# Moving the routing steps of the layer-1 context attention by one pair of heads

## The chip, the cores and the metric

The kernel runs on one core of a Trainium2 chip. The metric is the device time of one execution in microseconds (us), and the lower the better. Five engines work side by side, each taking its own instructions strictly in the order in which they were queued: TensorE (PE, matrix products, with its weight loads listed apart as PEld), VectorE (DVE), ScalarE (ACT), GpSimd (POOL) and SyncE (SP, which only starts transfers). They wait for each other through semaphores. The order on every engine is fixed when the kernel is built.

## The reference, cut to what matters

The program is a decoder of four layers (L0 to L3), each with a self-attention, a cross-attention to a context and a feed-forward part, on x of shape 8 batches x 256 rows x 256. The part that matters is the cross-attention of L1 and the beginning of what follows it:

```
q = x Wq + bq,  k = ctx Wk + bk,  v = ctx Wv + bv       # 16 heads of 64; ctx has 77 rows per batch
s = q k^T / 8,  masked keys replaced by a large negative number
p = softmax(s);  o = p v
x = layernorm(x + concat(o) Wo + bo)                     # the "new x" of the batch
# L1 feed-forward: a mixture of 8 experts, 2 per row, each with a limited capacity
r = rms-scaled x;  probs = softmax(r W_router);  top 2 of 8
rank of each row in its expert = number of earlier rows that chose that expert
rows with rank < capacity are scattered to their expert's slots
```

The routing of a batch needs that batch's new x, and, for the ranks, the counts of all batches before it.

## The kernel before

The cross-attention of L0 and of L1 is one function, `cross64` (L849); `bias` is true for L1 alone. It walks over the eight batches b = 0 to 7. A batch has two tiles of 128 rows (t = 0, 1) and eight pairs of heads (n = 0 to 7). For each batch it goes through these stages:

1. `weights(b)`: 64 matmul instructions on L919 make the scores of 16 heads. ScalarE copies them (L932), VectorE masks them (L933), takes the maximum (L939) and subtracts it (L940), ScalarE takes the exponential (L899), VectorE sums and inverts (L901, L902), and POOL (t = 0) or VectorE (t = 1) multiplies (L903). This is the tile P.
2. Three of the next batch's query projections q (L156, from xt and w), the values V of the batch (L156, from w and cT), and the output projection of the batch before (L156, from w and oT, two groups of 16 instructions). `finish` (L279) adds that to x (L281) and starts the layer norm: statistics (L253, L255), the inverse root on POOL (L183, L184), and the new tile x (L264).
3. `outputs(b)`: the loop over the eight pairs n. Each turn takes the next query projection if one is left (five turns have one, and in the last batch none), perhaps a "tick", the product po of the turned probabilities with V (L970), and the transposes of P for pair n + 2 (L955, four instructions), which ScalarE or VectorE copy into PT (L144 or L142). Two pairs are turned before the loop. oT and q are copied out with their bias by ScalarE (L151) and VectorE (L149) in turn.

Below, T(n) is the group of transposes for pair n, PT(n) its copy, q(n) the query projection taken in turn n, po(n) and oT(n) the product of turn n and its copy.

A tick advances the oldest entry of a list of generators. At the end of a batch `put_both` is put on that list, and it puts `Routing.batch` behind itself. So the four ticks of `outputs(b)`, for b = 1 to 7, do four things for batch b - 1, in this order:

- first tick: two transposes of each of the two tiles of the new x (L236), copied to xt by VectorE and ScalarE;
- second tick: the router's matmuls (L156, from rw and xt) and the chain of small operations behind them: scores (L2576), maximum (L2578), subtraction (L2579), exponential on ScalarE (L2580), sum (L2581), reciprocal (L2582), scaling (L2583), top values and their places (L2586, L2587, L2588), the one-hot rows rhot (L2594), their sum rsel (L2597) and the running counts rbefore (L2600);
- third tick: nothing, an empty step;
- fourth tick: the matmuls with the tiles `upper` and `onesb` (L156) that count the earlier rows, from rsel and rbefore, the ranks (L2609, L2611) and slots (L2615 to L2620), and four scatters on POOL (L1041).

The ticks stand ahead of the turn's po. In the first batch the list is empty, so nothing happens there.

The queue order is not the order of the text in every place: a scheduler chooses, at build time, where among the copies each small operation of VectorE and ScalarE stands. The squares for the root mean square (L2554), though issued by the second tick, stand far ahead of it on ScalarE.

## Time and profile before

| what | us |
|---|---|
| time, median of 3 runs | 3500.77 (3495.93 to 3503.63) |
| the profiled execution's own time | 3466.69 |
| its span, first to last instruction | 3465.0 |
| mean granted TensorE clock | 0.913 |
| one full batch of the L1 context attention, start of L919 to the next | 34.28 |
| TensorE busy in it | 32.63 |
| VectorE busy in it | 27.89 |

The profile is that of one execution, which was 34 us shorter than the median of the runs. Busy times of an engine count instructions in flight, and a TensorE that is shown busy may run at half clock; the granted clock stands beside it in the table of windows. Idle time is shown in square brackets with what ended it.

### The profile page before, as it was taken

How to read it: one execution, taken by the hardware profiler on the slowest of the kernel's cores; microseconds unless marked ns; L12 is line 12 of the kernel's file. 1: busy time of each engine (PE TensorE's matmuls, PEld its weight loads, DVE VectorE, ACT ScalarE, POOL GpSimd, SP SyncE). 2: the span in 40 equal slices, each digit the busy share in tenths (PEclk: the TensorE clock that was granted, in tenths of full speed). 3: DMA queues.
4: the chain of work that ended last, by engine and by line, in shares of the span. 5: the costliest groups of instructions: out<-in, count | busy, mean ns of one | idle time of the engine just before them, and what ended most of it. 6: DMA issues, size and time to landing. Idle time of an engine off the chain costs nothing. (4 is left out here: it accounts for less than half of the span.)

```text
span 3465.0 us, 49405 instructions
## 1 busy us (share of the span) xinstructions
PE 3068.0 (89%) x19135; PEld 2169.0 (63%) x19146; DVE 1819.0 (52%) x4852; ACT 1055.4 (30%) x2386; POOL 911.1 (26%) x1370
## 2 busy tenths in 40 slices
PE   4777679989998998998999999898888998888789
PEld 3444357768886666665566776565555886676556
DVE  7887556641005656785111221576675344777652
ACT  4666422222222233332111111343222112344211
POOL 2222323343313211232000000322343454322241
PEclk6777779989999999999999999999777999988899
DMA  9900110025532000001010333100002562000000
GB/s 334 333 1 6 34 42 16 16 94 185 187 128 89 17 28 14 17 17 59 14 37 25 113 131 118 37 20 8 7 19 84 200 210 77 25 1 7 13 6 19
DMA packets 132672, 241.58 MB, mean 70 GB/s; under 512 B 14600, under 2 KB 103952, under 8 KB 124752
## 3 DMA queue, kind: packets, MB, share of 16 engines
q1 hardware_dynamic: 108176, 138.34, 11.8%
q0 software_dynamic: 23104, 98.95, 8.3%
q8 instruction: 155, 2.54, 0.3%
q10 hardware_dynamic: 1152, 1.05, 0.1%
q14 instruction: 85, 0.70, 0.1%
HBM read 158.61 MB, written 79.69 MB: 69 GB/s over the span
## 5 line engine op out<-in xcount | busy, mean ns | idle before, releaser
L156 PE MATMUL ps<-xt,w 128*128 128x256 f32 (+1 forms) x1408 | 444.6, 465 | 8.3 <-issue 8.3
L156 PE MATMUL ps<-w,hT 128*128 128x256 f32 (+1 forms) x1792 | 397.4, 380 | 0.0
L156 PEld LDWEIGHTS ps<-w,hT 128*128 128x128 f32 (+1 forms) x1792 | 330.5, 187 | 55.9 <-issue 6.0
L156 PE MATMUL ps<-gT,w 128*128 128x256 f32 (+1 forms) x1472 | 356.9, 401 | 5.7 <-ACT gT L144 3.0
L156 PEld LDWEIGHTS ps<-xt,w 128*128 128x128 f32 x1408 | 263.8, 194 | 150.5 <-issue 129.8
L156 PEld LDWEIGHTS ps<-gT,w 128*128 128x128 f32 x1472 | 276.8, 191 | 76.1 <-ACT gT L144 3.9
L156 PE MATMUL ps<-w,oT 128*128 128x256 f32 x768 | 184.1, 394 | 12.3 <-DVE oT L1423 11.2
L156 PEld LDWEIGHTS ps<-w,oT 128*128 128x128 f32 x768 | 147.7, 196 | 48.6 <-issue 12.6
L1147 ACT ACTIVATE hT<-ps,more 128x256 f32<-128x256 f32 x152 | 71.9, 473 | 199.1 <-PE ps L156 199.1
L236 PE MATMUL ps<-ident,x 128*128 128x128 f32 x320 | 64.8, 314 | 74.2 <-DVE x L264 57.3
L276 POOL TENSOR_TENSOR xb<-x,rows 128x256 f32<-128x256 f32 x96 | 74.0, 778 | 212.7 <-DVE res L281 205.5
L264 DVE TENSOR_SCALAR x<-res,mv,rs 128x256 f32<-128x256 f32 x128 | 58.8, 459 | 123.0 <-POOL rs L184 123.0
L1158 DVE COPY y<-ps 128x512 f32<-128x512 f32 x41 | 28.3, 690 | 174.6 <-PE ps L156 174.6
L1224 DVE TENSOR_TENSOR hT<-hT,ps 128x512 f32<-128x512 f32 x56 | 38.5, 687 | 150.6 <-PE ps L156 150.6
L686 ACT ACTIVATE e<-ps,nm 128x128 bf16<-128x128 f32 (+1 forms) x256 | 103.7, 459 | 40.1 <-DVE nm L681 24.1
L1220 ACT ACTIVATE hT<-ps 128x512 f32<-128x512 f32 x56 | 33.4, 597 | 238.5 <-PE ps L156 238.5
L1717 POOL TENSOR_TENSOR kpad<-kpad,rows 128x256 f32<-128x256 f32 (+1 forms) x10 | 7.3, 729 | 363.5 <-DVE hu L1666 276.2
L236 PEld LDWEIGHTS ps<-ident,x 128*128 128x128 f32 x320 | 39.5, 155 | 98.9 <-DVE x L264 44.9
L903 POOL TENSOR_TENSOR P<-P,z 128x1232 f32<-128x1232 f32 (+1 forms) x32 | 55.2, 1734 | 167.3 <-DVE z L902 167.3
L970 PE MATMUL ps<-PT,V 77*64 77x256 f32 x512 | 90.8, 413 | 6.9 <-ACT PT L144 4.4
L1581 ACT ACTIVATE f<-ps,neg 128x512 f32<-128x512 f32 x128 | 77.3, 688 | 57.7 <-PE ps L1578 57.7
L1582 DVE SCALAR_TENSOR_TENSOR f<-ps,f 128x512 f32<-128x512 f32 x128 | 79.1, 682 | 26.1 <-ACT f L1581 26.1
(665 smaller groups left out, 6344.7 us busy)
## 6 DMA issues: line engine op xcount, KB each, us to landing
l2x<-zero SPq DMA_DIRECT2D x28, 1024.0 KB, 11.4
l0x<-zero SPq DMA_DIRECT2D x16, 1024.0 KB, 11.4
w<-in_L_ffn_rg SPq DMA_DIRECT2D x8, 1024.0 KB, 7.1
w<-in_L_ffn_ru SPq DMA_DIRECT2D x8, 1024.0 KB, 5.0
w<-in_L_ffn_rd SPq DMA_DIRECT2D x8, 1024.0 KB, 5.4
l2e<-y SPq DMA_DIRECT2D x22, 256.0 KB, 2.3
rows<-in_rows SPq DMA_DIRECT2D x9, 544.0 KB, 3.7
l0e<-y SPq DMA_DIRECT2D x19, 256.0 KB, 2.7
```

The lines of the kernel that those rows point to most:

```text
L156: self.nc.tensor.matmul(out, lhsT, rhs, start=(i == 0), stop=(i == last))
L236: self.nc.tensor.transpose(ps[:, k * P : (k + 1) * P], x[:, k * P : (k + 1) * P], self.ident)
L264: nc.vector.tensor_scalar(t, r, mv[:, 0:1], rs, ALU.subtract, ALU.mult)
L276: self.nc.gpsimd.tensor_tensor(t, self.X[i], row, ALU.add)
L686: nc.scalar.activation(e[:, : (t + 1) * P], ps[j][:, i, :], AF.Exp, bias=nm[:, t, h : h + 1], accum_out=z[:, t, h : h + 1],)
L903: eng.tensor_tensor(pr, pr, z.unsqueeze(2).to_broadcast([P, n, SC]), ALU.mult)
L970: nc.tensor.matmul(po[64 * m : 64 * m + 64, :S], V[:, h * 64 : (h + 1) * 64], ahead[n % 2][:, m, :], start=True, stop=True,)
L1147: nc.scalar.activation(hT[:, f + m, :], ps[:, m * 256 : (m + 1) * 256], func, bias=more[:, f + m : f + m + 1])
L1220: nc.scalar.activation(hT[:, f, :], ps, func, **({"bias": bias(f)} if bias else {}))
L1224: nc.vector.tensor_tensor(hT[:, f, :], hT[:, f, :], ps, ALU.mult)
L1581: nc.scalar.activation(f[:, j], ps[j], AF.Exp, bias=neg1)
L1582: self.mark = nc.vector.scalar_tensor_tensor(f[:, j], ps[j], 1.0, f[:, j], ALU.max, ALU.min)
```

## The change

The four ticks of a batch are taken in other turns of the loop in L1: turns 2, 4, 5 and 7 in the place of 1, 3, 5 and 7. L0 keeps its turns. The first and the second tick so come one pair later, the empty third and the fourth stay where they were.

```diff
@@ cross64, outputs
                 for n in range(8):
                     next(between, None)
-                    if n % 2:
+                    if n in ((2, 4, 5, 7) if bias else (1, 3, 5, 7)):
                         self.tick()
                     po = self.ps()
```

No instruction is added or removed. In the built order POOL's and SyncE's queues are the same as before; those of TensorE, ScalarE and VectorE differ in `outputs` of batches 1 to 7. The two copies to xt change engines (the first tile's goes to VectorE, the second's to ScalarE), since the copies take turns.

VectorE's queue from the router's scores to the counts, in batches 1 to 6, before and after:

```
before: L2576, oT(3), L2578, L2579, L2581, L2582, L2583, L2586, L2587, L2588, L2594, PT(6), L2597, PT(7), L2600, oT(6), L2600
after:  oT(3), L2576, L2578, L2579, PT(6), L2581, L2582, PT(7), L2583, oT(6), L2586, L2587, L2588, L2594, L2597, L2600, L2600
```

In batch 7, before and after:

```
before: L2576, L2578, PT(5), L2579, PT(6), L2581, L2582, PT(7), L2583, oT(6), L2586, L2587, L2588, L2594, L2597, L2600, L2600
after:  PT(5), L2576, L2578, PT(6), L2579, PT(7), L2581, oT(6), L2582, L2583, L2586, L2587, L2588, L2594, L2597, L2600, L2600
```

(The small steps for the experts' weights, L2630, L2633 and L2634, are left out here; they stand between L2587 and L2600.)

## The prediction

> **What bounds the kernel now.** I read the page first, then the table of windows by batch, then TensorE's waits in this stage, then the timeline of a middle batch and of the last one. The page and the window of batch 2 (the columns are PE, PEld, DVE, ACT, POOL busy, then granted clock and DMA):

> ```profile
> PE 3068.0 (89%) x19135; PEld 2169.0 (63%) x19146; DVE 1819.0 (52%) x4852; ACT 1055.4 (30%) x2386; POOL 911.1 (26%) x1370
> ...
> 1398.65:1432.93 34.28, 32.63 (x217) 23.42 (x217) 27.89 (x86) 13.25 (x30) 10.56 (x13) 1.00 0.05 17
> ```

> TensorE is busy for 32.63 of 34.28 us, at full clock, and no transfer matters (DMA share 0.05). So a batch costs what TensorE's queue costs. TensorE's waits from 1375 to 1606 us:

> ```profile
> PE ps L236 <- DVE x L264: 9.6, 6, 1.6
> PE ps L970 <- ACT PT L144: 4.4, 1, 4.4
> PE ps L156 <- DVE rsel L2597: 1.9, 1, 1.9
> ```

> The first line is what the change aims at: six batches in which the transposes of the new x wait 1.6 us for x. The third is one wait, in the last batch, for rsel. In the timeline of batch 2:

> ```profile
> 1419.02 0.66 DVE L142 COPY PT<-ps 77x512 f32<-77x512 f32 x1
> ...
> 1419.19 0.38 PE L236 MATMUL ps<-ident,x 128*128 128x128 f32 x2
> ...
> 1420.72 0.41 DVE L264 TENSOR_SCALAR x<-res,mv,rs 128x256 f32<-128x256 f32 x1 [0.95 <-POOL rs L184]
> ...
> 1421.19 0.44 PE L236 MATMUL ps<-ident,x 128*128 128x128 f32 x2 [1.61 <-DVE x L264]
> ...
> 1423.60 0.65 PE L970 MATMUL ps<-PT,V 77*64 77x256 f32 x4
> ...
> 1430.23 0.66 PE L955 MATMUL ps<-ident,P 128*77 128x128 f32 x4
> 1430.82 0.65 PE L970 MATMUL ps<-PT,V 77*64 77x256 f32 x4
> 1431.40 0.18 PE L156 MATMUL ps<-rsel,upper 128*128 128x8 bf16 x1
> ...
> 1432.93 3.80 PE L919 MATMUL ps<-l1kT,qT 64*128 64x77 f32 x64
> ```

> The first tile is ready and the second is 1.61 us late. The lines from 1430.23 are T(7), po(6), the counting matmul of rsel and the next scores: no wait there now. VectorE's rsel ended 0.59 us before its matmul (1430.65 + 0.16, against 1431.40).

> **What the change takes away.** Without the transposes, turn 1 goes on to po(1), T(3), q(2). They are 2.04 us apart per turn (1423.60 less 1421.56, po(2) less po(1) now). But po(1) needs PT(1), which VectorE copies from 1419.02 for 0.66 us, behind the first x and its statistics. TensorE would reach po(1) at 1419.19 and can start it at about 1419.74 (0.06 us for the semaphore, as from x's end at 1421.13 to 1421.19): a new wait of 0.55. Then T(3) at 1420.32, q(2) at 1420.82, the transposes at 1421.69. Both tiles have been ready since 1421.13, so they take 0.49 and po(2) starts at 1422.2, not 1423.60. The gain is 1.4 us on TensorE at this point. The two xt copies change engines; that costs nothing, for their readers, the router's matmuls, come two turns later (about 4 us).

> Going on, T(7) starts at 1430.23 - 1.4 = 1428.85, as router and pair 3 only change places.

> **What it adds.** The router's matmuls end as before plus one pair, and the counting matmul stays in turn 7. Between them TensorE now has po(4), T(6), po(5), T(7), po(6), about 2.9 us; before, po(3), T(5) and q(4) lay between as well, 2.04 us more. VectorE's queue for this is PT(6), L2581, L2582, PT(7), L2583, oT(6), L2586 and so on to L2597, and the in-order engine cannot start L2583 before T(7) is done and copied. That order has run already: from PT(7) to rsel it is the order of batch 7 before the change (T(7), PT(7), then VectorE's steps, then the counting matmul):

> ```profile
> 1599.65 0.66 PE L955 MATMUL ps<-ident,P 128*77 128x128 f32 x4
> ...
> 1600.35 0.69 DVE L142 COPY PT<-ps 77x512 f32<-77x512 f32 x1 [0.21 <-PE ps L955]
> 1600.96 0.16 DVE L2583 TENSOR_TENSOR rs<-rs,rm 128x16 f32<-128x16 f32 x1
> ...
> 1602.53 0.17 DVE L2597 TENSOR_TENSOR rsel<-rhot 128x16 bf16<-128x16 f32 x1
> ...
> 1602.77 0.18 PE L156 MATMUL ps<-rsel,upper 128*128 128x8 bf16 x1 [1.87 <-DVE rsel L2597]
> ```

> T(7) to counting matmul: 1602.77 - 1599.65 = 3.12 us, with 1.87 us of TensorE idle. Taken over, the counting matmul comes at 1428.85 + 3.12 = 1431.97, against 1431.40: every batch from 1 to 6 loses 0.57 us net, having gained 1.4 and lost 1.97. Behind that wait stand po(7) and the 64 score instructions; ScalarE and VectorE wait for these, and the whole softmax of the next batch hangs on them, so the loss is carried one for one. Six batches: 3.4 us. POOL's four scatters start after the slots and follow; POOL then waits another 4.04 us for L903's input (1408.96), so they stay covered; uncovered, four of 1.27 us would show. In batch 7 no x was late; there L2582 and L2583 now stand behind oT(6), two dependent steps of about 0.2 us more: 0.4. Sum at full clock: +3.8 us.

> **The clock.** These windows of 3.41 us are TensorE busy, granted clock, DMA:

> ```profile
> 1557.19:1560.61 3.42, 2.29 (x14) 1.00 0.00 0
> ...
> 1601.57:1604.98 3.41, 2.21 (x12) 1.00 0.00 0
> 1604.98:1608.39 3.41, 3.41 (x10) 0.50 0.11 38
> ...
> 2434.42:2437.83 3.41, 3.41 (x40) 0.50 0.00 0
> 2437.83:2441.25 3.42, 1.98 (x40) 0.50 0.02 5
> ```

> The clock changes only at the edges of such windows. The first row holds most of an x wait and is followed by full clock; the second holds the end of the rsel wait, tiny matmuls and po(7), and half clock follows. Busy time alone does not tell them apart. Weighting each matmul's streaming time by its rows over 128 does: in the first row projections and transposes fill 0.58 of the window, in the second po(7) has 77 rows and the counting matmuls stream 8 columns, 0.35. Over all windows of this trace at full clock, I get no fall above about 0.42 beyond a few strays, and hardly any stay below 0.36. The other way, the fourth row is full of work and the clock does not return: half of it is 32-row matmuls. By the same sum, windows at half clock return above about 0.75. All these shares are my estimates, from instruction shapes and start times.

> For the new wait: a window with 1.9 us idle keeps 1.5 us for T and po (about 0.8 by this measure) or po(7) and L919 (about 0.45 to 0.5), so 0.15 to 0.35, mostly a fall. It takes effect near the start of L919. L919 has 64 rows, so by the estimate it cannot bring the clock back; 3.8 us of scores become 7.6, and only a window of projections, V and output projection ends it. That is two or three windows, 6.8 to 10.2 us at half clock, so 3.4 to 5.1 us lost. Of this 0.55 comes back, since TensorE then reaches PT(1) late. TensorE carries the rest, not VectorE: the first half of P was ready at 1412.7 (L903, 1411.93 + 0.78), 2.7 us before T(0) at 1415.4. With 2.5 windows: 4.25 - 0.55 = 3.7 per batch; for six batches 22, if nearly all fall.

> [...] The 1601.57 row shows a fall with at most 1.9 us idle in one piece, so I go by the row.

> **Sum.** 3.8 + 22 = +26 us. The profiled execution would go from 3466.69 to about 3493. The median of the runs is 34 us longer for reasons the profile doesn't show; I add the same 26 to it: 3500.8 + 26 = 3527.

> **Rivals.**
> - *The clock falls for one window only, or seldom.* If L919's pairs count as full activity, one window costs 1.7 - 0.55 = 1.15 us; with the 3.8: +10.7, about 3511. With no fall at all +3.8, about 3505. For it: the six x waits of 1.6 us never cost the clock. Against: those stand among 128-row projections, the new wait between 77-row and 64-row work.
> - *Faster.* The rsel chain costs nothing new, because TensorE's next po's and VectorE's copies move apart enough. Then 1.4 us times six is gained: -8.4, about 3492. It decides for faster where the new wait is under 1.4 us. Against: the queue order and the 3.12 us above, of which over 1 us are ten small operations that cannot overlap.
> - *The change doesn't remove the wait*, since the second x is late for turn 2 too. It would need x 0.6 us later than now; then about +11 with no fall in clock, near the first rival.

> **How the numbers follow.** Lasting fall of the clock 0.62. It gives from 3.8 + 3 x 2.85 = +12 (half of the six batches fall, for two windows) to 3.8 + 6 x 5.1 = +34 (all fall, for three windows, and nothing comes back). One window or seldom, +3.8 to +12, 0.25; faster 0.10; the rest 0.03. The range from 3503 to 3538 takes both of the first two cases, with 1 us below and 3 above for the spread of the runs (3495.93 to 3503.63), and leaves out the faster one. A measurement of this kernel tells about 0.2%, 7 us. Slower by more: 0.62 and 0.16 of the 0.25. Within: the other 0.09 and the 0.03. Faster: 0.10.

> **What would show it.** After: TensorE's waits list x (L264) no longer for L236 in six batches, PT(1) some 0.5 us each for L970 if the batch was not slowed, and rsel seven times near 1.9 us. The windows after each show 0.50 under L919, and its instructions last near 7 us. A batch lasts about 38.5 us, not 34.28. I am wrong on the clock if L919 stays at 3.8 us, and wrong on the chain if rsel waits are under 1.4 us.

## The result and the profile after

The change makes the kernel slower: 3523.68 us median of 7 runs (3510.92 to 3528.57) against 3500.77 for the kernel before, ratio 1.0065 [1.0049, 1.0082], or +22.9 us. The profiled execution took 3523.71 us (span 3522.0, mean granted clock 0.898, against 0.913).

The line of the page with the busy times, which answers to that of before:

```profile
PE 3121.0 (89%) x19135; PEld 2202.5 (63%) x19146; DVE 1817.7 (52%) x4852; ACT 1056.0 (30%) x2386; POOL 911.5 (26%) x1370
```

The window of the same batch in the kernel after, from one start of L919 to the next (columns as before):

```profile
1409.01:1449.36 40.35, 38.48 (x217) 28.18 (x217) 28.01 (x86) 13.24 (x30) 10.77 (x13) 0.84 0.04 14
```

The instructions are the same (217 matmul instructions in both windows; VectorE, ScalarE and POOL are busy as long as before to within 0.3 us), but TensorE is busy for 38.48 us instead of 32.63, at a mean clock of 0.84 instead of 1.00. The batch lasts 40.35 us; of the four that follow three take 40.48 to 40.65 and the last 38.65. TensorE's waits from 1375 to 1660 us (total, times, longest):

```profile
PE ps L156 <- DVE rsel L2597: 13.4, 7, 2.2
PE ps L970 <- ACT PT L144: 2.2, 1, 2.2
PE ps L970 <- DVE PT L142: 0.3, 1, 0.3
```

The line for x is gone, and rsel is waited for seven times instead of once. TensorE's timeline around the end of a batch:

```profile
1396.35 0.60 PE L236 MATMUL ps<-ident,x 128*128 128x128 f32 x4
...
1404.10 0.65 PE L970 MATMUL ps<-PT,V 77*64 77x256 f32 x4
1406.62 0.19 PE L156 MATMUL ps<-rsel,upper 128*128 128x8 bf16 x1 [1.87 <-DVE rsel L2597]
...
1406.80 1.12 PE L970 MATMUL ps<-PT,V 77*64 77x256 f32 x2
...
1409.01 7.11 PE L919 MATMUL ps<-l1kT,qT 64*128 64x77 f32 x64
```

All four transposes of x run in one piece without a wait. The counting matmul waits 1.87 us, and from there on everything takes about twice as long: each of the two groups of po(7) 1.12 us instead of 0.65, the 64 score instructions 7.11 us instead of 3.80. The windows of 3.41 us at the end of the next batch (TensorE busy, clock, DMA) show where the clock goes and when it is back:

```profile
1443.65:1447.06 3.41, 1.54 (x15) 1.00 0.00 0
1447.06:1450.48 3.42, 3.42 (x18) 0.50 0.00 0
...
1460.71:1464.13 3.42, 3.42 (x10) 1.00 0.03 3
```

The first row holds the rsel wait; half clock follows for four windows, 1447.06 to 1460.71. That the clock changes only at such edges holds for both traces: its 135 changes in the kernel before and its 149 in the kernel after lie on one even grid of 3.413 us, none more than 0.01 us off it.

### The profile page after: what moved, and what is told of

It is laid out like the page before. It is cut to its first block, busy times and chain, and to the rows that moved or that the text cites. A ratio compares the mean times of both kernels' runs of the same rounds, so it can differ in the third digit from the quotient of the medians.

```text
span 3522.0 us, 49419 instructions
## 1 busy us (share of the span) xinstructions
PE 3121.0 (89%) x19135; PEld 2202.5 (63%) x19146; DVE 1817.7 (52%) x4852; ACT 1056.0 (30%) x2386; POOL 911.5 (26%) x1370
## 5 line engine op out<-in xcount | busy, mean ns | idle before, releaser
L156 PE MATMUL ps<-xt,w 128*128 128x256 f32 (+1 forms) x1408 | 455.4, 474 | 7.7 <-issue 7.7
L156 PE MATMUL ps<-w,hT 128*128 128x256 f32 (+1 forms) x1792 | 397.4, 379 | 0.0
L156 PEld LDWEIGHTS ps<-xt,w 128*128 128x128 f32 x1408 | 270.7, 199 | 152.8 <-issue 128.9
L156 PE MATMUL ps<-gT,w 128*128 128x256 f32 (+1 forms) x1472 | 357.2, 400 | 9.9 <-issue 3.9
L156 PEld LDWEIGHTS ps<-w,hT 128*128 128x128 f32 (+1 forms) x1792 | 329.9, 186 | 56.5 <-issue 6.0
L156 PEld LDWEIGHTS ps<-gT,w 128*128 128x128 f32 x1472 | 276.1, 191 | 81.4 <-issue 4.3
L156 PE MATMUL ps<-w,oT 128*128 128x256 f32 x768 | 185.6, 396 | 12.2 <-DVE oT L1423 11.1
L156 PEld LDWEIGHTS ps<-w,oT 128*128 128x128 f32 x768 | 148.5, 197 | 49.3 <-issue 14.1
L236 PE MATMUL ps<-ident,x 128*128 128x128 f32 x320 | 62.0, 307 | 65.1 <-DVE x L264 48.1
L264 DVE TENSOR_SCALAR x<-res,mv,rs 128x256 f32<-128x256 f32 x128 | 56.6, 443 | 118.8 <-POOL rs L184 118.8
L1224 DVE TENSOR_TENSOR hT<-hT,ps 128x512 f32<-128x512 f32 x56 | 38.5, 687 | 149.8 <-PE ps L156 149.5
L970 PE MATMUL ps<-PT,V 77*64 77x256 f32 x512 | 98.2, 435 | 7.6 <-DVE PT L142 5.3
L903 POOL TENSOR_TENSOR P<-P,z 128x1232 f32<-128x1232 f32 (+1 forms) x32 | 55.2, 1734 | 182.4 <-DVE z L902 155.2
L236 PEld LDWEIGHTS ps<-ident,x 128*128 128x128 f32 x320 | 39.0, 153 | 87.7 <-issue 40.4
```

What stands on the lines that cost most here:

```text
L156: self.nc.tensor.matmul(out, lhsT, rhs, start=(i == 0), stop=(i == last))
L236: self.nc.tensor.transpose(ps[:, k * P : (k + 1) * P], x[:, k * P : (k + 1) * P], self.ident)
L264: nc.vector.tensor_scalar(t, r, mv[:, 0:1], rs, ALU.subtract, ALU.mult)
L903: eng.tensor_tensor(pr, pr, z.unsqueeze(2).to_broadcast([P, n, SC]), ALU.mult)
L970: nc.tensor.matmul(po[64 * m : 64 * m + 64, :S], V[:, h * 64 : (h + 1) * 64], ahead[n % 2][:, m, :], start=True, stop=True,)
L1224: nc.vector.tensor_tensor(hT[:, f, :], hT[:, f, :], ps, ALU.mult)
```

## The experiments

They ran in three sets. Each kernel is compared with runs of the kernel before made in the same set; the medians of these were 3495.3, 3470.8 and 3496.4 us. So the level differs between sets by 25 us, and profiles are compared within a set where that matters. "Stretch" below is the time from one start of L919 to the next; stretch b starts with the scores of batch b (0 to 6). The ticks of `outputs(b)` lie in stretch b, so the change bears on stretches 1 to 6, and a half clock that begins at the end of one runs on into the next (above, from 1447.06 to 1460.71 across the start of scores at 1449.36). The code is shown against the kernel after.

**Each half of the change alone.** First the x transposes only (`first_only`), in set 1:

```
-    if n in ((2, 4, 5, 7) if bias else (1, 3, 5, 7)):
+    if n in ((2, 3, 5, 7) if bias else (1, 3, 5, 7)):
```

> Ticks in turns 2, 3, 5, 7: of the change only the first part is kept (the transposes of the new x one pair later); router and counting stay where they were before. My theory: the x move alone is a gain. TensorE's waits lose the six of 1.6 us for x, rsel's wait stays a single one of about 1.9 us in batch 7, and the granted clock stays at 1.00 through the middle of the stage. A batch takes 34.28 - 1.4 = 32.9 us, the stage is 8 us shorter than before, and the ratio to the kernel before is about 0.9976. Rival A (moving the transposes is itself the harm, through new waits for PT or for the copies of xt): batches of 38 us and more and a ratio near that of the change, 1.006. Rival B (any shift against the clock's windows costs, whichever part is moved): half-clock windows appear in this stage too, ratio above 1.

Measured: ratio 0.9977 [0.9961, 0.9992], faster. The x wait is gone, there is no half clock between batch 1 and batch 6. Stretches 2 to 6 take 33.86 to 33.91 us, not 32.9: PT(1) is waited for six times, 7.1 us in all, up to 1.4, where I had put 0.55. Rivals A and B fall. Stretch 3 (columns as before):

```profile
1441.64:1475.50 33.86, 32.48 (x217) 23.41 (x217) 27.97 (x86) 12.92 (x30) 10.56 (x13) 1.00 0.05 17
```

Then the later router only (`second_only`), in set 1:

```
-    if n in ((2, 4, 5, 7) if bias else (1, 3, 5, 7)):
+    if n in ((1, 4, 5, 7) if bias else (1, 3, 5, 7)):
```

> Ticks in turns 1, 4, 5, 7: of the change only the second part is kept (router and softmax of the routing one pair later); the transposes of the new x stay in turn 1. My theory: this part carries the whole loss. The six x waits of 1.6 us are there, the rsel wait of 1.87 us is there in every batch, the clock falls in it and stays at 0.50 for three or four windows through the scores, whose 64 instructions take about 7 us. A batch is as long as after the change plus the 1.4 us that the first part had saved: 40.5 + 1.4 = 41.9 us where four windows fall, ratio to before about 1.009. Rival A (the x move is the harm): ratio 1.000, batches of 34.3 us.

Measured: ratio 1.0073 [1.0052, 1.0094]: this half alone costs as much as the whole change. But stretches 2 to 5 are 40.1 to 40.6 us as after the change, not 41.9, and x is waited for once (1.5 us) instead of six times. TensorE's waits from 1375 to 1620 us:

```profile
PE ps L156 <- DVE rsel L2597: 11.2, 6, 1.9
PE ps L236 <- DVE x L264: 1.5, 1, 1.5
```

The score instructions have a median of 0.414 us here, against 0.272 in the kernel before, so TensorE reaches the transposes later, and five of the six times it waits for nothing there. So the gain of the x move was not there to be taken in these stretches, and the two halves do not add.

**Filling the wait** (`filled`, set 1). Turn 7, in front of the tick, in batches 1 to 7 (the condition that picks them is left out here; each of the four matmuls is two instructions in the timeline):

```
+    self.mm(self.ps()[:, :S], [(self.ident, self.cT[:, 0, :S])] * 4)   # result unused
```

> The kernel after, with four matmuls of 128 rows by 256 columns (the identity against part of the context, into a PSUM tile that nobody reads) put in front of the counting matmul in turn 7 of batches 1 to 7. They add about 1.7 us of TensorE work just where TensorE waits 1.87 us for rsel; nothing else is changed, the counting matmul starts no earlier. My theory (the wait costs mostly because the clock falls in it): the clock stays at 1.00 through the scores, which take 3.8 us again in place of 7.1; a batch takes 34.28 + 0.6 = 34.9 us instead of 40.5, and the kernel is some 30 us faster than the kernel after, ratio to before 1.000 to 1.003, although it does more work. Rival (the scores are slow for another reason, such as what VectorE or ScalarE do beside them, and the clock has no part): no gain; the time stays that of the kernel after, ratio 1.006 or above.

Measured: ratio 0.9999 [0.9983, 1.0014], with more work than the kernel after and 0.7% less time. TensorE's waits from 1375 to 1575 us, and a middle stretch:

```profile
PE ps L970 <- DVE PT L142: 7.1, 6, 1.4
```

```profile
1444.39:1480.09 35.70, 34.34 (x225) 24.85 (x225) 28.11 (x85) 12.90 (x30) 10.57 (x13) 1.00 0.05 16
```

The clock column reads 1.00, and the stretch 35.70 us in place of 40.5. The filler ends at the moment rsel is ready (1442.96 us), so the counting matmul is no earlier than it would be with the wait. What is saved is the clock alone.

**Filling it with few rows** (`filled16`, set 2): the same four matmuls of 16 rows.

```
+    self.mm(self.ps()[:, :S], [(self.ident[:16, :], self.cT[:16, 0, :S])] * 4)
```

> The kernel after with four matmuls in front of the counting matmul, as in the kernel that filled the rsel wait, but of 16 rows by 256 columns in place of 128 by 256: TensorE is kept just as busy (about 1.9 us), with an eighth of the rows. My theory (what the clock follows is streaming weighted by rows): it falls as after the change, the scores take about 7 us, a batch 40.5 us, ratio to before 1.006. Rival (idle time in one piece of more than about 1.9 us is what drops the clock): no fall, batches of 35.7 us as with 128 rows, ratio 1.000.

Measured: ratio 1.0081 [1.0065, 1.0097], stretches 2 to 5 of 40.3 to 40.6 us: no better than the change. TensorE's timeline, then two of its clock windows:

```profile
1438.57 1.99 PE L156 MATMUL ps<-cT,ident 16*128 16x256 f32 x8
...
1442.89 7.12 PE L919 MATMUL ps<-l1kT,qT 64*128 64x77 f32 x64
```

```profile
1437.07:1440.48 3.41, 3.41 (x20) 1.00 0.00 0
1440.48:1443.89 3.41, 3.41 (x19) 0.50 0.00 0
```

The first window has no idle time at all, and half clock follows. So it is not idling that drops the clock here. 128 rows kept it (`filled`, 1.00), a row count of 16 did not (0.50).

**Filling half of it** (`filled2`, set 2): two matmuls of 128 rows instead of four.

> The kernel after with two instead of four matmuls of 128 rows by 256 columns in front of the counting matmul: about 0.95 us of the rsel wait stays. My estimate of the share (0.15 to 0.35 of a window without filling, plus 0.95 / 3.41 = 0.28) is 0.43 to 0.63, above the bound near 0.36: no fall, a batch takes 35.7 us, since the counting matmul still waits for rsel, ratio 1.000. Rival (any wait of some 0.9 us among these 77-row and 64-row matmuls drops the clock): batches near 40.5 us, ratio 1.006; half of the windows falling would give about 38 us.

Measured: ratio 1.0021 [1.0008, 1.0034], in between. Its waits from 1360 to 1560 us and a stretch:

```profile
PE ps L156 <- DVE rsel L2597: 4.0, 5, 0.8
PE ps L970 <- DVE PT L142: 1.4, 4, 0.4
```

```profile
1438.49:1473.23 34.74, 33.54 (x222) 24.10 (x221) 28.03 (x86) 13.04 (x30) 10.57 (x13) 1.00 0.05 17
```

In stretches 3 to 5 the clock holds (34.71 to 34.74 us, 1.00), in stretches 2 and 6 it falls for three windows (39.2 us, mean clock 0.87 in stretch 2). The same program keeps or loses the clock, and the difference that I find between these stretches is where the windows lie. By the sum of the prediction (streaming time weighted by rows over 128, an estimate from instruction shapes and start times) the windows that ended in a fall have a share of 0.33 (one of them is 1396.97 to 1400.39, TensorE busy for 2.61 of 3.42 us), so the bound near 0.36 held here; my share of 0.43 to 0.63 was wrong, since such a window begins only about where the filler ends, with the wait, po(7) and scores in it. At full clock the stretch is 34.73, PT(1) waits 0.4: here these two are as I had predicted (34.28 + 0.57 and 0.55).

**Counting behind the next scores** (`late_count`, set 1):

```
-    if n in ((2, 4, 5, 7) if bias else (1, 3, 5, 7)):
+    if n in ((2, 4, 5) if bias else (1, 3, 5, 7)):
...
-    Pt = weights(b + 1, self.q_next)
+    Pt = weights(b + 1, self.q_next); bias and self.tick()
```

> The kernel after, with the counting matmuls moved from turn 7 to behind the scores of the next batch (in the last batch to the end of the stage); no work added or left out. My theory: rsel is ready long before TensorE comes to it, so the wait of 1.87 us is gone as well as that for x; the clock stays at 1.00, and a batch takes 34.28 - 1.4 = 32.9 us, like the kernel that moves x alone: ratio to before about 0.9976. If the wait at full clock were the only cost (no part of the clock), the gain over the kernel after would be 7 x 1.9 = 13 us: ratio 1.0028. Rival (the counting and the scatters in front of POOL's and VectorE's softmax work hold up the next batch's weights): a new wait for P or PT in front of T(0), batch of 34.3 us or more.

Measured: ratio 1.0041 [1.0024, 1.0058]. The rsel wait is gone, as expected, but stretches 2 to 6 are 38.1 to 39.4 us: a new wait took its place, though not at P. TensorE waits for x ten times, 20.3 us, up to 3.6. POOL's timeline tells why:

```profile
1420.90 1.09 POOL L1041 DMA_INDIRECT l1x<-x,rto  x1 [6.07 <-DVE rto L2620]
...
1424.83 0.96 POOL L1041 DMA_INDIRECT l1x<-x,rto  x1 [0.30 <-issue]
1425.87 0.19 POOL L183 TENSOR_SCALAR rs<-mv 128x1 f32<-128x1 f32 x1
```

The four scatters, 1.27 us apart, now stand on POOL in front of the layer norm's inverse root (L183, L184), which x waits for. In the prediction I had priced scatters that are "uncovered" at 1.27 us each; this is that case, with the clock falling in the long x wait on top (3.56 us up to 1428.38, and po(2) behind it takes 1.12 us instead of 0.65). So this run does not give the price of the rsel wait by itself; `filled` does that for the clock.

**The kernel before again** (`before_2`, set 2), since its first profile was 34 us below its median.

> The kernel before, unchanged, profiled once more. Open is why its first profiled execution took 3466.69 us where its median is 3495 to 3501. My theory: that execution met fewer half-clock windows than usual outside the middle of the stage. The four profiles of the kernels changed so far all show 37 to 41 us of half clock in 1310 to 1680 us where their batches 1 to 6 have none, against 20.5 us in the first profile of before, and 132 to 149 us after 2700 us. So a second profile should last 3485 to 3505 us, the batches should be 34.28 us again, and the half clock at the start and in batch 7 should be some 35 us. Rival: in usual runs the x wait of 1.6 us costs the clock as well, so that the batches themselves are longer than 34.28 us (36 or more).

Measured: 3461.19 us, and stretches of 34.28 us, with 20.5 us of half clock from 1310 to 1680 us: the first profile over again. My theory was wrong; the kernel before is simply that fast in this set (3459.26 to 3480.04). The four kernels with more half clock at the end of the stage do not stand for the kernel before.

**PT(1) on ScalarE** (`pt1_act`, set 2), on top of the x move:

```
-    ahead = [turned(Pt, 0), turned(Pt, 1)]
+    ahead = [turned(Pt, 0), turned(Pt, 1, bias)]      # copied by ScalarE, other copies as before; the part in `turned` is left out here
```

> The kernel that moves only the transposes of x (turns 2, 3, 5, 7), with the copy of PT(1) on ScalarE instead of VectorE, every other copy where it was. In the kernel that moves x alone the batch fell only to 33.87 us, not 32.9, for a wait of 1.38 us for PT(1) instead of 0.55. My theory: PT(1) stands on VectorE behind the first x and its statistics, and VectorE starts the batch 1.0 us later against TensorE than before; ScalarE is idle there (from 1425.78 to 1428.88), so the wait goes, x is late for its transposes by 0.2 to 0.8 us instead, and a batch takes 32.7 to 33.3 us: ratio 0.995 to 0.997. Rival (VectorE's own queue is now what a batch lasts by, about 33.9 us): the wait moves to a later PT or to P at the start of the batch, and the batch stays at 33.9 us, ratio 0.9977 as with x alone.

Measured: ratio 0.9968 [0.9953, 0.9982], the lowest ratio of all, though its interval overlaps that of the x move alone. Stretches are 32.45 us, a little better than I expected: from 1360 to 1560 us TensorE has no listed wait at all, not even for x. VectorE, freed of one copy, makes the second x 0.46 us earlier after the start of the scores than in the kernel before (22.02 against 22.48 us).

**Before, x alone and after side by side** (set 3). In set 1, ScalarE's copies of the scores had stood for up to 1.9 us with nothing to wait for, in set 2 not.

> The kernel before, unchanged, profiled a third time. The kernels with x alone moved and with the filled wait, both run on a first chip, show ScalarE's copies of scores (L932) standing 1.3 and 1.9 us after their matmuls were done, in five batches, while the scatters run; the kernels run on a second chip (the second profile of before, two fillers, PT(1) on ScalarE) show none of it. Theory: this stall belongs to the chip, not to the change. If this run is on a chip with the stall, VectorE is about 1 us later against TensorE, the x wait is near 2.6 us instead of 1.6 and a batch of the kernel before lasts 35.2 us, not 34.28; then the profile is some 3490 us or more, and the loss of the change on such a chip is about 7 us less than the profiles of before suggest. On a chip without it: 34.28 us again, 3459 to 3480 us. Rival (the stall comes with the moved transposes): 34.28 us here even where the kernel with x alone, run beside it, shows the stall.

> The kernel with only x moved (turns 2, 3, 5, 7) once more, beside the kernel before on the same chip. Where ScalarE's copies do not stall: PT(1) waits 0.4 to 0.55 us, as I had predicted, and a batch takes 32.8 to 32.9 us. Where they stall: PT(1) waits 1.38 and a batch takes 33.87 us, as in the first profile. Rival (the longer wait for PT(1) is the change's own, on any chip): 33.87 us on both.

> The kernel after once more, on the same chip as the third profile of before, to set batch against batch. My theory: batches 1 to 6 about 40.4 us with four half-clock windows in most, rsel waits of 1.87, and batch 7 some 7 us longer than in the kernel before, since there the fall of the clock in the wait for PT(0) lasts seven windows instead of two. Where the profiles of both kernels are of the same chip, their difference should come to the ratio of the runs, 1.0065 to 1.0085. Rival: the batches differ as before by 37 us but the medians by 23 again, and the rest is won back in a later stage.

Measured, the kernel before: 3495.96 us. Two of its stretches:

```profile
1407.25:1442.52 35.27, 32.85 (x217) 23.31 (x216) 27.99 (x86) 13.15 (x30) 10.56 (x13) 1.00 0.05 16
1442.52:1479.40 36.88, 34.48 (x217) 24.22 (x216) 27.97 (x86) 13.15 (x30) 10.56 (x13) 0.95 0.05 15
```

and ScalarE's timeline in the first:

```profile
1408.78 1.26 ACT L932 COPY P<-ps 128x308 f32<-128x308 f32 x3
1411.50 0.42 ACT L932 COPY P<-ps 128x308 f32<-128x308 f32 x1 [1.46 <-PE ps L919]
...
1414.51 0.74 ACT L932 COPY P<-ps 128x308 f32<-128x308 f32 x2 [1.87 <-PE ps L156]
```

TensorE's scores were done by 1411.1 us, yet the last copies start at 1414.51. So the stall is not the change's own: the kernel before has it too, in set 3. Nor does it go by the chip, as I had thought: sets 2 and 3 ran on the same chip, set 1 on another. The x waits of the kernel before are then 0.4 and 1.9 us in a batch, together 2.4 instead of 1.6, and TensorE is busy for 0.2 us more, which makes 35.27 us; in stretches 3, 4 and 6 the clock falls for a window as well, and they take 36.8 to 36.9.

`first_only_2`: 3477.64 us, stretches 2 to 6 of 33.85 to 33.90 us with PT(1) waiting 1.4, as expected for a set with the stall. Against 35.27 the x move gains 1.38 us a batch at full clock.

`after_2`: ratio 1.0076 [1.0059, 1.0092]. Its profiled execution was the shortest of its runs (3506.17 of 3506.17 to 3530.82), and its stretches 2 to 6 take 37.52 to 37.53 us, not 40.4, with two windows at half clock, not four:

```profile
1443.08:1446.50 3.42, 2.64 (x30) 1.00 0.00 0
1446.50:1449.91 3.41, 3.41 (x38) 0.50 0.21 76
...
1453.32:1456.74 3.42, 3.42 (x14) 1.00 0.00 0
```

Here the window that holds the end of the rsel wait ends at 1446.50, some 1.2 us into the scores; in the first profile it ends at 1447.06, before po(7) and all scores. That is the difference that I find between 37.5 and 40.5 us. In this profile the half clock begins at 1408.95, 1446.50, 1484.04 and so on, 11 windows or 37.55 us apart: just a stretch, so every batch meets the windows in the same place. The rival of this run partly holds too: the profiles of set 3 differ by 10.2 us and the medians by 24.0. With the first profile of after, which is a median run (3523.71), the difference to the third of before, also near its median, is 27.8 us: stretches 0 to 6 of the stage together +21.0 (246.2 to 267.2), batch 7 and what follows up to L1572 +6.9 (622.4 to 629.3), all else about 0.

## Why the prediction was right, step by step

The total was right (+26 forecast, +22.9 and +24.0 measured), and so was its cause. Not every term was, and that the total came so near is in part luck, since some errors cancel.

- *The x wait goes, 1.4 us a batch.* Right where it could be seen by itself: 1.38 us (`first_only_2` against `before_3`). After the change the gain is not there, since half clock takes it back (`second_only` costs the same without it).
- *PT(1) waits 0.55.* Right in a set without the stall on ScalarE (0.4, `filled2`), 1.4 with it. VectorE is then about 1 us later in the batch (the first x starts 20.29 us after the start of the scores in `first_only`, 19.28 in the kernel before). In the kernel after, PT(1) waits once for 0.3, as foreseen for a slowed batch.
- *The counting matmul waits 1.87 to 1.97, net +0.57.* Right: 1.87 in batches 1 to 6, and 34.73 - 34.28 = +0.45 net at full clock.
- *The clock falls and the scores cannot bring it back.* Right: filling the wait with full rows kept the clock and took back 4.8 us a stretch (40.5 to 35.7), and in both profiles of after the half clock lasted past the last score (1447.06 to 1460.71, with the scores done by 1456.48; 1446.50 to 1453.32, done by 1451.32). The row that I went by is confirmed: a wait of 1.87 us was followed by half clock here, and `filled16` lost the clock with no wait at all. The bounds on the share are less sharp than I had them: by the same sum, again an estimate, a window with a share of 0.47 ended in a fall (after, 1402.69 to 1406.10) and one with 0.43 did not (`filled2`, 1506.20 to 1509.61).
- *Two or three windows, 3.7 us a batch: the term mis-sized.* The first profile shows four, 40.48 - 34.73 = 5.75 us a stretch, the other two, 37.53 - 34.73 = 2.8. I had counted the windows under the scores, but not that the fall comes ahead of po(7) there (1447.06), nor that the window of projections after which it is over (1457.30 to 1460.71) is itself run at half clock (0.50).
- *"The six x waits never cost the clock": wrong.* True of the profile that I had; in `before_3`, whose time is that of a typical run of its set, three of six did. So the price of the old x wait was higher than 1.4 us there, and the kernel before loses to its own clock what I took for a plain baseline. This offsets the term above: stretches 0 to 6 cost +21.0 against a typical run, where the first two profiles alone would say 267.2 - 236.6 = +30.6.
- *Batch 7, +0.4: wrong, +6.9.* The rsel wait of this batch grew by 0.3 us (1.87 to 2.19), about as forecast; the rest is the clock. It falls in or just behind TensorE's wait for PT(0) (4.4 us in the kernel before, half clock from 1587.91; 2.2 in the kernel after, half clock from 1631.38). In the three profiles of the kernel before it was back after two windows (1594.74 in the first); in the ten of changed kernels once after two (`first_only_2`), else after five to eight (`first_only` eight, the kernel after seven in both, in the first at 1655.27). Both happened to one and the same kernel, so the order of its instructions alone does not decide it; whether the change makes the long return likelier, these runs do not settle. Nor does the prediction's bound of 0.75 for a return explain it: by the same sum, an estimate too, the first of the seven windows in the kernel after (1631.38 to 1634.79) has 0.92 and did not end the half clock.
- *The 34 us between the profile and the median.* I left them unexplained and added the same +26 to both. The sets show what they are: the level of before moves by 25 us from set to set, the profile was taken at the level of set 2, the timed runs at that of sets 1 and 3. Between the first and the third profile of before, 9.7 us lie in stretches 0 to 6, where the stall and its clock falls are; the rest lies in other stages (8.6 us ahead of the first scores, and from L1572 to the end 1273.4 us in the first profile, 1283.5 in the third), and its cause stays open.

Of the rivals, "one window or seldom" happened in part of `filled2`, not in the kernel after. "Faster" needed an rsel wait under 1.4 us and got 1.87. "The wait isn't removed" did not occur.

## What to carry to other kernels

Where a wait is moved, ask what work stands around it: 1.6 us among 128-row projections cost only itself (in the two profiles that had it so; with 0.4 and 1.9 us, in the third, it took the clock in three of six batches), 1.87 us in front of 77-row and 64-row work cost 2.8 to 5.8 us more through the clock. Judge a reordering by the parts it is made of, on the chip: here one half gains 0.23% and the other loses 0.73%, and the half that gains, with one copy on another engine, gains 0.32%. And before reading a gain out of two profiles, see whether the profile of the baseline is like its timed runs; here it was one of a faster level.
